# Another order of query tiles in a causal first pass, and weights before rows in the late expert slots of a decoder kernel

## The chip, the cores and the metric

The kernel runs on one core of a Trainium2 chip. A core has five engines with instruction streams of their own: TensorE (PE, matrix products; its weight loads are listed as PEld), VectorE (DVE), ScalarE (ACT), GpSimd (POOL) and SyncE (SP), which mostly issues DMA transfers. The streams are tied together by semaphores. The metric is the device time of one execution in microseconds, the median over runs.

## The reference, cut to what matters

Two decoder layers over `x` of shape 4 x 512 x 256, in float32. Layer 0: an attention over landmarks, an attention block, a quantised linear map. Layer 1: a hyperbolic attention, two further attentions with their own feed-forward nets, and a mixture of experts. Two pieces are touched by the change. The first is the causal half of layer 0's attention block (16 heads, queries and keys of 16 numbers, padded to 32 in the kernel):

```python
att = jnp.einsum('bhqd,bhkd->bhqk', q, k) * scale
causal = jnp.tril(jnp.ones((T, T), bool))
att = jnp.where(causal[None, None], att, -jnp.inf)
y = jnp.einsum('bhqk,bhkd->bhqd', jax.nn.softmax(att, axis=-1), v)
```

The second is the mixture of experts, in which each of 2048 tokens has its two best of eight experts:

```python
for e in range(NUM_EXPERTS):
    h = jax.nn.gelu(x @ W1[e] + b1[e])
    y = h @ W2[e] + b2[e]
    output = output + y * combine_w[..., e:e + 1]
```

## The kernel before, in words

**Attention as a stream of steps.** `Stream` (its `run`) works through *units*: one batch, one group of four heads, one kind. A unit has two passes. The first pass (`d_tile`) takes a tile of 128 queries against the keys (L386) and lets VectorE reduce the row maxima (L394 for causal units, L398 for the others). The second pass (`a_tile`) computes the scores again with keys as rows, the maxima already subtracted (L421), exponentiates them on ScalarE (L422) into `pt`, and a step later `outputs` multiplies them by the values (L517). One step of the stream holds one first-pass tile of one unit, one second-pass tile of an earlier unit, and the output products of the step before, in two halves. In a half, two heads of the first pass and two of the second are written out alternately; each head occupies 32 rows of TensorE, so the four stand in different row groups. The scores lie in a ring of seven PSUM banks.

In a causal unit the work narrows. Query tile `qt` of the first pass is `(qt + 1) * 128` keys wide; key tile `i` of the second pass is `512 - 128 * i` queries wide, with `i` from 0 to 3. Each batch of layer 0 has four cross units (eight steps, all 512 wide) and then four causal units (four steps each). The cross units set the distance between the passes: the second pass of a causal unit runs ten steps after its first pass. So of a batch's 16 causal steps of a first pass, ten meet a second pass of a cross unit and six meet one of a causal unit. Between them lie small pieces of work (projections, transposes, layer norms), placed by a planner with costs and due times; it doesn't look at widths.

**Experts by slots.** Tokens are scattered into `rows`, sorted by expert, by GpSimd's indirect DMAs (L1653). The products then go over 39 *slots* of 128 rows with one expert each. Slots 0 to 15 (`NEARLY = 16`) can be fixed once three batches are known, the other 23 only at the end, from a second table `tab1`. A slot needs its weights (`fetch_w`, L1809: 2052 KB into a pool of four buffers) and its rows (`fetch_z`, L1803: 128 KB into a pool of 16). `turn` transposes the rows (L1820, copied by L1822), `hidden` computes half of the first product (L1831) with its GELU (L1833), `output` the second product (L1838), which VectorE copies into `ys` (L1840) and SP stores (L1841). Before each fetch SP reads the expert or the row number from the table into a register.

`begin` asks for weights and rows of slots 0 to 2 and for rows of slots 3 to 15. Then `round` lays, for slot `s`: `fetch(s + 3)`, `hidden(s + 1)` twice, `turn(s + 2)`, `output(s)`. Rounds 0 to 12 are laid by `begin`, rounds 13 to 38 by `rest`, a second chain. The first piece of `rest`, `fetch(16)`, has no cost for the planner and is laid as soon as the second chain exists, in the middle of round 5. All these transfers are issued by SP, in program order on one queue; an instruction on SP that waits holds up those behind it. Order on TensorE is program order as well.

Of the kernel before, what the change touches and what calls it, by code (L numbers as in the profile page):

```python
# [23 lines left out]
NT = T // P  # L24
# [5 lines left out]
NEARLY = 16  # L30
VW = 16 * 17 + 15
NSLOT = 2 * B * T // P + E - 1
# [5 lines left out]
def decoder_kernel(ctx: ExitStack, tc: tile.TileContext, a: dict, out: bass.AP):  # L38
# [3 lines left out]
    def ts(i, n=P):  # L42
        return slice(i * n, (i + 1) * n)
# [34 lines left out]
    def ring():  # L78
        return banks["s"].tile([P, 512], F32, name="ps_s", tag="s")
# [227 lines left out]
    class Stream:  # L307
# [69 lines left out]

        def d_tile(self, u, i, j):
            if u.mode == "causal":
                qt, hf = NT - 1 - i, 0  # L380
                n = (qt + 1) * P
            else:
                qt, hf, n = i // u.halves, i % u.halves, 512
            r = ts(j, 32)
            ps = ring()
            PE.matmul(ps[:, 0:n], u.qT[r, ts(qt)], u.kT[r, hf * 512 : hf * 512 + n], start=True, stop=True)  # L386
            m = u.mx[:, qt, j, hf : hf + 1]
            if u.norm:

                V.tensor_reduce(m, ps[:, 0:n], AX.X, ALU.max, negate=True)  # L390
                self.open.append((ps[:, 0:n], m, u.sm[:, qt, j, hf : hf + 1]))
            elif u.mode == "causal":
                junk = self.one.tile([P, T], F32, name="junk", tag="junk")
                V.tensor_tensor_reduce(  # L394
                    junk[:, 0:n], ps[:, 0:n], self.dmask[:, T - n : T], 1.0, NEG, ALU.add, ALU.max, m
                )
            else:
                V.tensor_reduce(m, ps[:, 0:n], AX.X, ALU.max)  # L398
# [611 lines left out]
    def l1_attn(wo, spk, qk_d, v_d, left, done):  # L1010
        with ExitStack() as st:
# [173 lines left out]
            with tc.manual_schedule():  # L1185
                fetch(0, 0)
                n = len(units)
                prev_o = None
                for i in range(-1, n + 2):
                    u = units[i] if 0 <= i < n else None  # L1190
                    p = units[i - 1] if 0 <= i - 1 < n else None
                    nx = units[i + 1] if 0 <= i + 1 < n else None
                    if nx and nx.qts[0] == 2 and i >= 0:
                        k = 2 * nx.b + nx.hh + 1
                        if k < 2 * B:
                            fetch(k // 2, k % 2)
                    if p:
                        squares(p)
                    if u:
                        roots(u)  # L1200
                        pump()
                    if nx:
                        scores(nx)
                    if prev_o:
                        finish(*prev_o)
                        prev_o = None
                    if p:
                        prev_o = (p, outputs(p))
                    if u:
                        logs(u)  # L1210
# [474 lines left out]
    class Slots:  # L1685
# [123 lines left out]
            nc.sync.dma_start(u.w, a["we"][bass.ds(ex, 1)].rearrange("o p n -> p (o n)"))  # L1809

        def fetch(self, s):
            u = self.us[s]
            if s >= NEARLY:
                self.fetch_z(u)
            self.fetch_w(u)

        def turn(self, u):
            ps = ring()
# [203 lines left out]
```

## Time and profile before

| What | us |
|---|---|
| Median of 3 runs (lowest, highest) | 3512.26 (3512.18, 3515.68) |
| The profiled execution's own time | 3505.88 |
| Its span | 3504.0 |
| PE busy (share of the span) | 3055.5 (87%) |
| DVE busy | 2107.0 (60%) |
| ACT busy | 1901.9 (54%) |
| POOL busy | 781.5 (22%) |
| Causal first passes on VectorE (L394), first to last | 326.1 to 1081.4 |
| First fetch of an expert slot | 3093.3 |
| First and last product of the slots (L1831, L1838) | 3103.8, 3455 |

Times in the profile are microseconds from the start of the span. A row of the time line has start and length, the engine, the line of the kernel, the operation, what it writes and reads, and in brackets how long the engine had been idle and whose work ended that. Rows of PE are single hardware passes; a float32 product is two of them, so 32 passes of L1831 are the 16 products of both halves of `hidden`. SPq is SP's own queue: its rows are the issue of a transfer, and the landing is told apart. "PEclk" is the share of full clock that TensorE was granted.

### The profile page before, as it was taken

What the parts mean: (1) busy time and instruction counts of PE and PEld (TensorE: products, weight loads), DVE (VectorE), ACT (ScalarE), POOL (GpSimd) and SP (SyncE); (2) the same over time, 40 slices, a digit from 0 to 9 for tenths busy, and PEclk for the clock granted to TensorE, in tenths of its full rate; (3) what the DMA queues carried; (4) which work ended last, traced back from release to release, by engine and by line L of the source; (5) the groups of instructions that cost most, each with busy time, mean ns of one, the idle gap of its engine ahead of it and who ended that gap; (6) DMA issues with size and microseconds to landing.
All of it is one profiled execution on the core that took longest, in us unless ns stands there. A gap on an engine that the chain in (4) does not pass through costs nothing.

```text
span 3504.0 us, 50650 instructions
## 1 busy us (share of the span) xinstructions
PE 3055.5 (87%) x19095; PEld 1489.4 (43%) x19095; DVE 2107.0 (60%) x5076; ACT 1901.9 (54%) x3845; POOL 781.5 (22%) x667
## 2 busy tenths in 40 slices
PE   6689999999998576677899999999998998987994
PEld 3433333333333344344434444433333333457894
DVE  4576676776765677876776565655646656532112
ACT  2235555454553865879587667465663655532231
POOL 1010112122022745677222121100102001011003
PEclk9789999999999567777899999999998999999997
DMA  8100000010001100110000000000000000045895
GB/s 281 59 24 7 1 7 3 6 31 4 11 19 41 56 1 32 54 69 7 25 1 1 1 19 1 7 13 19 13 1 13 7 1 19 1 164 208 290 328 168
DMA packets 81397, 176.08 MB, mean 50 GB/s; under 512 B 6264, under 2 KB 63744, under 8 KB 76032
## 3 DMA queue, kind: packets, MB, share of 16 engines
q1 hardware_dynamic: 76016, 161.16, 13.1%
q0 software_dynamic: 3072, 8.39, 0.8%
q8 instruction: 150, 2.46, 0.3%
q10 hardware_dynamic: 2064, 3.29, 0.3%
q14 instruction: 95, 0.78, 0.1%
HBM read 127.48 MB, written 45.34 MB: 49 GB/s over the span
## 4 chain that ended last, share of the span: by engine, by line
PE 66%; DVE 13%; ACT 7%; issue 7%; DMA 5%; POOL 2%; SPq 0%; ACTq 0%; DVEq 0%; POOLq 0%
PE ps_s L386 16%; PE ps_g L517 7%; PE ps_s L421 5%; PE ps_s L661 3%; PE ps_s L1831 3%; PE ps_s L1838 3%; PE ps_s L1410 3%; PE ps_s L1356 3%; PE ps_s L1426 3%; PE ps_s L414 2%; PE ps_s L1145 2%; PE ps_g L524 2%; DMA rows<-ln_z,idx 1%; PE ps_s L1367 1%; DMA we<-in_we 1%
## 5 line engine op out<-in xcount | busy, mean ns | idle before, releaser
L422 ACT ACTIVATE pt<-ps_s 128x512 f32<-128x512 f32 (+2 forms) x1536 | 791.0, 569 | 749.0 <-PE ps_s L421 647.8
L386 PE MATMUL ps_s<-kT,qT 32*128 32x512 f32 (+3 forms) x3072 | 921.9, 623 | 45.6 <-ACT pt L422 28.0
L398 DVE TENSOR_REDUCE mx<-ps_s 128x1 f32<-128x512 f32 x768 | 489.3, 683 | 222.0 <-PE ps_s L386 124.8
L386 PEld LDWEIGHTS ps_s<-kT,qT 32*128 32x128 f32 x3072 | 310.9, 186 | 338.5 <-issue 96.4
L390 DVE TENSOR_REDUCE mx<-ps_s 128x1 f32<-128x512 f32 x512 | 328.3, 684 | 194.1 <-PE ps_s L386 190.9
L421 PE MATMUL ps_s<-qa,kT 32*128 32x512 f32 (+3 forms) x1536 | 436.0, 590 | 4.9 <-ACT pt L422 3.1
L421 PE MATMUL ps_s<-qT,kT 32*128 32x512 f32 x1536 | 417.6, 636 | 0.0
L402 ACT ACTIVATE ps_s<-ps_s,mx 128x512 f32<-128x512 f32 x512 | 340.9, 670 | 32.8 <-DVE mx L390 32.3
L1833 ACT ACTIVATE hid<-ps_s,we 128x128 f32<-128x128 f32 x312 | 88.9, 368 | 221.4 <-PE ps_s L1831 144.5
L1105 POOL TENSOR_TENSOR s<-s,mh 128x1280 f32<-128x1280 f32 x64 | 187.1, 2948 | 76.9 <-ACT mh L1104 57.1
L394 DVE CUSTOM_DVE_ANT_0 junk<-ps_s,dmask 128x512 f32<-128x512 f32 (+3 forms) x256 | 125.2, 489 | 95.8 <-PE ps_s L386 52.9
L1831 PE MATMUL ps_s<-zsT,we 128*128 128x128 f32 x1248 | 148.8, 278 | 22.7 <-DMA we<-in_we 20.6
L1088 PE MATMUL ps_s<-qk 32*128 32x256 f32 (+3 forms) x512 | 105.3, 628 | 65.6 <-DVE mh L1093 55.3
L421 PEld LDWEIGHTS ps_s<-qa,kT 32*128 32x128 f32 x1536 | 143.8, 185 | 42.7 <-DVE mx L398 24.0
L414 PE MATMUL ps_s<-qm,all 3*128 3x512 bf16 x768 | 156.6, 387 | 5.8 <-ACT ps_s L402 3.1
L164 POOL TENSOR_TENSOR ln_r<-ln_ve,mhalf 128x4 f32<-128x4 f32 x40 | 40.8, 1020 | 538.4 <-DVE ln_ve L159 476.0
L1831 PEld LDWEIGHTS ps_s<-zsT,we 128*128 128x128 f32 x1248 | 146.5, 194 | 28.0 <-issue 19.2
L1120 POOL TENSOR_TENSOR s<-s 128x1280 f32<-128x1280 f32 x64 | 147.6, 2337 | 12.3 <-ACT s L1116 12.3
L1147 DVE COPY pt<-ps_s 128x512 f32<-128x512 f32 x160 | 108.3, 687 | 58.7 <-PE ps_s L1145 58.7
L1145 PE MATMUL ps_s<-ident,s 128*128 128x128 f32 x640 | 127.7, 336 | 16.6 <-ACT s L1139 15.3
L1838 PE MATMUL ps_s<-we,hid 128*128 128x256 f32 x624 | 141.0, 379 | 0.0
L1093 DVE TENSOR_SCALAR_CACHE_REDUCE mh<-ps_s 128x512 f32<-128x512 f32 (+3 forms) x256 | 108.5, 486 | 53.1 <-PE ps_s L1092 28.8
(439 smaller groups left out, 5117.5 us busy)
## 6 DMA issues: line engine op xcount, KB each, us to landing
we<-in_we SPq DMA_DIRECT2D x39, 2052.0 KB, 8.8
rows<-zero SPq DMA_DIRECT2D x8, 2048.0 KB, 16.8
qk_d<-qkT SPq DMA_DIRECT2D x32, 256.0 KB, 2.7
qk<-qk_d SPq DMA_DIRECT2D x8, 1024.0 KB, 6.5
zs<-rows SPq DMA_DIRECT2D x39, 128.0 KB, 3.6
outs<-ys SPq DMA_DIRECT2D x39, 128.0 KB, 4.2
li<-in_a_li SPq DMA_DIRECT2D x4, 1024.0 KB, 8.7
v_d<-vp SPq DMA_DIRECT2D x16, 143.5 KB, 1.8
```

The source lines that it names most:

```text
L386: PE.matmul(ps[:, 0:n], u.qT[r, ts(qt)], u.kT[r, hf * 512 : hf * 512 + n], start=True, stop=True)
L390: V.tensor_reduce(m, ps[:, 0:n], AX.X, ALU.max, negate=True)
L398: V.tensor_reduce(m, ps[:, 0:n], AX.X, ALU.max)
L402: S.activation(ps, ps, AF.Exp, bias=m, accum_out=sm)
L414: PE.matmul(ps, self.ones[r, :], u.qm[r, :], start=True, stop=False)
L421: PE.matmul(ps[:, c0:], u.kT[r, ts(kt)], (u.qa if u.first_row else u.qT)[r, c0:], start=u.first_row, stop=True)
L422: S.activation(u.pt[:, j, c0:], ps[:, c0:], AF.Exp, scale=u.scale)
L517: PE.matmul(o[r, c0:], u.v(kt, j), pt[:, j, c0:], start=first, stop=last)
L1105: G.tensor_add(s, s, m)
L1145: PE.transpose(ps[:, ts(j)], u.s[h // 2][:, h % 2, c0 : c0 + P], ident)
L1831: PE.matmul(ps[:, ts(f)], u.w[:, k : k + P], u.zT[:, c, :], start=c == 0, stop=c == 1)
L1838: PE.matmul(ps[:, 0:C], u.h[:, f, :], u.w[:, 2048 + f * C : 2048 + f * C + C], start=f == 0, stop=f == 7)
```

## The change

In a causal unit, the first pass takes query tiles in the order 1, 0, 3, 2 instead of 3, 2, 1, 0, so its widths are 256, 128, 512, 384 instead of 512, 384, 256, 128. Ten steps later the second pass of that unit has 512, 384, 256, 128; in the steps where two causal units meet, both passes are now equally wide.

In the experts' stage, `fetch(s)` asks for the weights of slot `s` first. Then, for late slots only, it asks for the rows of slot `s - 1`; the call for the last slot asks for the rows of slots 37 and 38. The first call for a late slot, `fetch(16)`, asks for no rows at all: rows 16 come with weights 17.

```diff
         def d_tile(self, u, i, j):
             if u.mode == "causal":
-                qt, hf = NT - 1 - i, 0
+
+                qt, hf = (1 - i) % NT, 0
                 n = (qt + 1) * P
...
         def fetch(self, s):
-            u = self.us[s]
-            if s >= NEARLY:
+
+            self.fetch_w(self.us[s])
+            for u in self.us[max(s - 1, NEARLY) : s + (s == NSLOT - 1)]:
                 self.fetch_z(u)
-            self.fetch_w(u)
```

## The prediction

> **What bounds the kernel now.** I read the page first (busy tenths by slice), then the time line and the landings of the expert stage (3101 to 3457 us), then SP's waits, then the time line of the causal steps. TensorE is busy in nine tenths of most slices, and the DMA row rises only at the end:
>
> ```profile
> PE   6689999999998576677899999999998998987994
> DMA  8100000010001100110000000000000000045895
> ```
>
> In the rounds that handle late slots (16 to 38) nothing but TensorE sets the pace. Stretch of 160 us, columns: length, busy time of PE, PEld, DVE, ACT, POOL, granted clock, DMA share, GB/s:
>
> ```profile
> 3277.20:3437.30 160.10, 159.71 (x1100) 150.31 (x1101) 24.04 (x74) 50.21 (x176) 0.00 (x0) 1.00 0.89 320
> ```
>
> PE is busy 159.71 of 160.10 us: 22 rounds of 7.28 us. One of them on the time line:
>
> ```profile
> 3343.14 3.73 PE L1831 MATMUL ps_s<-zsT,we 128*128 128x128 f32 x32
> 3343.34 0.42 DVE L1840 COPY ys<-ps_s 128x256 f32<-128x256 f32 x1 [3.03 <-PE ps_s L1838]
> 3343.80 0.33 SPq L1841 DMA_DIRECT2D outs<-ys  x1
> 3344.91 0.34 SPq L1803 DMA_DIRECT2D zs<-rows  x1
> 3346.09 0.34 SPq L1809 DMA_DIRECT2D we<-in_we  x1
> 3346.71 0.38 PE L1820 MATMUL ps_s<-ident,zs 128*128 128x128 f32 x2
> 3346.93 3.62 PE L1838 MATMUL ps_s<-we,hid 128*128 128x256 f32 x16
> ```
>
> Call this round s. TensorE runs hidden(s+1), the row transposes turn(s+2), output(s). SP, once ys of slot s-1 is copied (3343.76), stores it, then asks for rows s+3 (1.15 us after the copy) and weights s+3 (2.33 us after). Rows s+3 are wanted a whole round later, so today their landing is hidden.
>
> **The change, part 1: late fetches.** The four compute engines execute the same instructions in the same order; SP issues as many, reordered. Round s now asks for weights s+3 first and then for rows **s+2**, which turn(s+2) wants in the same round. How long does a row transfer take behind a weight transfer? The first slots show it, from the views of the two tiles (weights issued at 3096.9, rows at 3098.0):
>
> ```profile
> L1809 SPq DMA_DIRECT2D we<-in_we x1: 338/338/338, 3096.9 to 3096.9; - x1
> DMA to landing us min/median/max: 12.7/12.7/12.7
> L1803 SPq DMA_DIRECT2D zs<-rows x1: 338/338/338, 3098.0 to 3098.0; - x1
> DMA to landing us min/median/max: 11.8/11.8/11.8
> ```
>
> Weights land at 3109.6, rows at 3109.8. The next rows, issued 1.1 us behind the next weights, land 0.4 us after them (3115.2 against 3114.8), and stores issued 0.4 us behind weights land 0.3 to 0.4 us after them (3245.4 against 3245.0). So 128 KB behind 2 MB land about 0.35 us after it; with nothing in front they take 1.9 to 2.1 us. Weights into an empty queue land after 7.7 to 9.5 us, mean 8.54.
>
> A rule of the Trainium skill speaks against me: "DMA: Bandwidth & Descriptors", section on queues, rings and completion order, says that completion on one issuing engine's queue isn't first in, first out. By it the rows could land after their own 2.0 us: copy 0, rows issued 2.33, landed 4.3, wake-up 0.1, then turn to end of copy 4.29: a round of 8.7 us, 22 x (8.7 - 7.3) = +31 us. By the rows above it is: weights issued 1.15, landed 9.69, rows 10.04, wake-up 0.1, plus 4.29 (turn start to end of the ys copy: 3353.96 to 3358.25 for the next slot) = 14.43 us a round, 22 x (14.43 - 7.31) = +157 us. I take the rows: this case has the very pair of transfers in the very order. Queued behind the waiting turn(s+2) is output(s); behind that the ys copy, its store, and on SP the next weights, which is why the wait isn't made up later. 7.31 is my count of the same 22 rounds in the trace (ends of copies 3277.0 to 3437.95).
>
> Which rounds: rows 16 are asked for with weights 17 in round 14, rows 37 with weights 38 in round 35: **22 stalled turns**; rows 38 follow at once.
>
> **The clock.** Each round leaves TensorE idle from the end of hidden(s+1) (3.0 us after the copy) to 10.1: 7.1 us. What such a gap does:
>
> ```profile
> 3212.00:3217.00 5.00, 0.00 (x0) 0.00 (x0) 0.42 (x1) 0.00 (x0) 0.00 (x0) 1.00 0.77 249
> 3217.20:3226.90 9.70, 0.01 (x1) 0.04 (x1) 0.00 (x0) 0.00 (x0) 0.00 (x0) 0.50 0.95 384
> 3226.90:3230.70 3.80, 3.80 (x18) 3.80 (x19) 0.00 (x0) 0.00 (x0) 0.00 (x0) 0.50 0.97 416
> ```
>
> The granted clock falls to 0.50 some 5 us into the gap and stays there 3.8 us after work resumes; the 32 hidden matmuls then took 5.67 us where 3.73 is usual. The ten gaps of over 4.3 us from 1987 us on all end in half clock, which lasts 3.2 to 9.0 us after resumption, mean 5.1. The rule in "TensorE: Matmul & The Clock Gate" (Part 1) counts a warm-up of about 3.4 us: 1.7 us lost per round, 22 x 1.7 = +37. By the rows' mean it is 2.5 us, +56. I take the rows, and round to the grid they show: switches lie 3.41 us or multiples of it apart, and half clock lasts one filled interval after the next switch point. As half of that is added to the round, the phase settles where a round is a whole number of intervals: five, 17.07 us (14.43 + 2.64; the rows' ends are 1.6 and 4.5, but for nine of the ten gaps 3.3). Late rounds: **22 x (17.07 - 7.31) = +215 us.**
>
> **What part 1 takes away.** Slot 16's fetch is laid early, in round 5, and today its rows wait for the last scatter of tokens, with everything on SP behind them:
>
> ```profile
> SPq L1803 <- DMA rows<-ln_z,idx: 19.6, 1, 19.6
> ```
>
> ```profile
> 3226.89 5.67 PE L1831 MATMUL ps_s<-zsT,we 128*128 128x128 f32 x32 [14.90 <-DMA we<-in_we]
> ```
>
> Behind them stood weights 16, the stores of ys 5 to 7 and weights 9 to 11; TensorE ran out of weights (14.90). Now only weights 16 stand there; they need output(5) (done 3195.4). Weights 9 go as soon as output(6) ends, 3204.75, land 3213.3, and hidden(9) starts at 3213.4, not 3226.9, without the half clock. What is late next: weights 16 hold one of four buffers, so slots 9 to 15 still cycle through three, each asked for at the end of an output and needed 7.44 us later against 8.54 to land. Stepping through gives hidden(15) at 3261.4 instead of 3277.2: **-15.8 us** (bounds -17 and -13, by weights landing in 8.3 or 9.0).
>
> **The change, part 2: causal order.** First-pass widths go from 512, 384, 256, 128 to 256, 128, 512, 384. The second pass lags ten steps, so only 6 steps of each batch pair two causal passes; elsewhere the partner is 512 wide. Row groups run side by side, so half a step costs the wider of its two:
>
> ```profile
> 380.34 0.69 PE L386 MATMUL ps_s<-kT,qT 32*128 32x512 f32 x1
> 380.34 0.48 PE L421 MATMUL ps_s<-qa,kT 32*128 32x256 f32 x1
> 381.40 0.85 PE L517 MATMUL ps_g<-pt,vs 128*32 128x384 f32 x8
> 384.70 0.58 PE L386 MATMUL ps_s<-kT,qT 32*128 32x384 f32 x1
> ```
>
> The half with 512 and 256 lasts 1.06 us (380.34 to 381.40), one with 384 and 128 lasts 0.85. Output blocks of 512, 384, 256 and 128 columns take 1.07, 0.85, 0.64 and 0.43 us: 0.21 per 128 columns. Paired 256 with 256 and 128 with 128, two steps of a batch lose 0.42 in each of two halves: 1.7 us, four batches 6.8. PE is busy 69.0 of 69.0 us there, so it counts. VectorE keeps up barely: 4 x 0.84 us in a 512 step, 0.71, 0.57, 0.44 in the others; the wide step now falls where PE has little else to do (3.2 us). I take **-4.5 us**, bounds -7 (no new wait) and +2 (0.4 us more waiting in the widest step of each of 16 units).
>
> **Sum.** -15.8 - 4.5 + 215 = +194.7 us. The profiled execution took 3505.88 us (span 3504.0, 1.9 around it), so 3700.6; the runs' median is 6.4 above it: **3707 us**.
>
> **Rivals.** (a) No clock loss, if the gate bridges 7 us: +157 - 20.3, **3649**; against it stands every gap over 4.3 us after 1987. (b) Rows pass the weights: +31 - 20.3, **3523**; against it stand the landings. (c) The other side: rows not only pass but land before TensorE has finished hidden(s+1), and the two gains remain: 3512.3 - 20.3 = **3492**. It decides at a loss of 20.3 / 22 = 0.92 us a round, that is at rows landing 1.6 us after issue; the shortest of the trace is 1.92. (d) Worse: weights landing in 9.5 us, or half clock for 2 us longer a round: rounds of 18 to 19 us, 22 x (10.7 to 11.7) - 20.3: **3727 to 3750**.
>
> **How the numbers follow.** Queue order with half clock 0.78, its own range 3683 to 3728; (a) 0.07; (b) 0.05; (c) 0.02; (d) 0.08. The range goes down to (a) and ends between the likeliest case and the bulk of (d): 3645 to 3732. Faster by over 0.2% (7 us, about what a measurement of this kernel can tell) has only (c): 0.02; within it, between (b) and (c): 0.02; slower 0.96.
>
> **What would show it.** Right: rows landing within 0.5 us of weights; turn waiting about 7 us on the rows' transfer in 22 rounds; rounds near 17 us, clock about 0.8 in that stretch; no 19.6 us wait before weights 16; PE halves of 0.64 and 0.43 in two causal steps per batch. Wrong: rows landing 2 to 3 us after issue, rounds of 14.4 us at full clock, or SP issuing weights ahead of ys.

## The result, and the profile after

The changed kernel takes **3694.15 us** (median of 6 runs, 3691.97 to 3702.73), the kernel before 3513.51 us (6 runs, 3511.41 to 3516.5): a ratio of 1.0516, interval 1.0503 to 1.053. The forecast was 3707 us, its range 3645 to 3732.

The page of the changed kernel, busy tenths in 40 slices and the granted clock:

```profile
PE   6699999999996676778999999999989898966553
PEclk9799999999996677778999999999999999987776
DMA  7200000000002001200000000000000004553343
```

The clock's row of the kernel before:

```profile
PEclk9789999999999567777899999999998999999997
```

The large differences lie in the last five slices (a slice is a fortieth of the span, 92 us here and 88 before, so the others shift a little). There TensorE, at 8, 7, 9, 9, 4 tenths before, falls to 6, 6, 5, 5, 3; the clock, at 9 before the last slice, falls to 8, 7, 7, 7, 6; and DMA, at 4, 5, 8, 9, 5 before, to 5, 3, 3, 4, 3. Nothing replaces TensorE as the bound: every engine waits. (Line numbers of the changed kernel are one higher than before from L386 on: turn L1821, hidden L1832, output L1839, copy of `ys` L1841, rows L1804, weights L1810.)

The same 22 rounds as in the prediction, from the copy of slot 13 to that of slot 35; columns: length, busy time of PE, PEld, DVE, ACT, POOL, granted clock, DMA share, GB/s:

```profile
3262.10:3626.40 364.30, 216.09 (x1102) 189.47 (x1101) 24.64 (x75) 50.37 (x176) 0.00 (x0) 0.75 0.40 144
```

PE executes the same matmuls (1102 here, 1100 before) in 364.30 us instead of 160.10. It is busy for 216.09 of them, against 159.71: the 56.4 us on top are the same products at half clock. The other 148.2 us are one and the same wait, once in each of the 22 rounds, as the group of the turn shows (busy time and mean ns, then idle time before and its releaser):

```profile
L1821 PE MATMUL ps_s<-ident,zs 128*128 128x128 f32 x78 | 21.1, 364 | 148.2 <-DMA zs<-rows 148.2
```

One round on the time line, the columns as before:

```profile
3376.71 3.73 PE L1832 MATMUL ps_s<-zsT,we 128*128 128x128 f32 x32
3376.91 0.42 DVE L1841 COPY ys<-ps_s 128x256 f32<-128x256 f32 x1 [5.41 <-PE ps_s L1839]
3377.36 0.33 SPq L1842 DMA_DIRECT2D outs<-ys  x1
3378.55 0.34 SPq L1810 DMA_DIRECT2D we<-in_we  x1
3379.66 0.34 SPq L1804 DMA_DIRECT2D zs<-rows  x1
3386.72 0.66 PE L1821 MATMUL ps_s<-ident,zs 128*128 128x128 f32 x2 [6.28 <-DMA zs<-rows]
3387.18 6.40 PE L1839 MATMUL ps_s<-we,hid 128*128 128x256 f32 x16
...
3393.61 0.42 DVE L1841 COPY ys<-ps_s 128x256 f32<-128x256 f32 x1 [5.77 <-PE ps_s L1839]
```

Copy ends at 3377.33, weights are asked for 1.2 us later, rows 2.3 us later; hidden is through at 3380.44, the turn starts at 3386.72, and the output products take 6.40 us where they took 3.62. The next copy ends at 3394.03: a round of 16.7 us, 7.2 before.

How long the two transfers take, from the views of the two tiles in these rounds; first the weights, then the rows:

```profile
L1810 SPq DMA_DIRECT2D we<-in_we x22: 337/338/348, 3263.3 to 3610.6; - x22
...
DMA to landing us min/median/max: 7.6/8.2/10.0
```

```profile
L1804 SPq DMA_DIRECT2D zs<-rows x23: 337/338/412, 3264.4 to 3612.8; - x23
...
DMA to landing us min/median/max: 6.8/7.3/8.0
```

Rows are issued 1.1 us behind the weights and take 0.9 us less: they land right behind them. In the 16 rounds of which the trace has both landings, rows land 0.29 to 0.35 us after the weights. By the ends of the copies, 22 rounds take 364.35 us (16.56 each) where they took 160.94 (7.32).

SP's waits between 3180 and 3262 us, while the slots 4 to 13 run (total, times, longest), which before held the 19.6 us on the scatter of tokens:

```profile
SPq L1810 <- PE ps_s L1839: 51.3, 8, 8.0
SPq L1842 <- DVE more L1698: 6.0, 1, 6.0
```

The wait on the scatter is gone; the longest of 8 us is at L1810, for a free weight buffer. The group of hidden between 3195 and 3262 us, first of the kernel before, then of the changed one:

```profile
L1831 PE MATMUL ps_s<-zsT,we 128*128 128x128 f32 x199 | 25.6, 290 | 17.7 <-DMA we<-in_we 17.7
```

```profile
L1832 PE MATMUL ps_s<-zsT,we 128*128 128x128 f32 x261 | 31.1, 277 | 6.0 <-DMA we<-in_we 6.0
```

TensorE waits 6.0 us for weights there instead of 17.7, and completes 261 single passes instead of 199.

Causal steps of the first batch, TensorE alone, in the changed kernel:

```profile
378.96 0.48 PE L387 MATMUL ps_s<-kT,qT 32*128 32x256 f32 x1
378.97 0.48 PE L422 MATMUL ps_s<-qa,kT 32*128 32x256 f32 x1
...
379.61 0.85 PE L518 MATMUL ps_g<-pt,vs 128*32 128x384 f32 x8
...
382.48 0.37 PE L387 MATMUL ps_s<-kT,qT 32*128 32x128 f32 x1
382.49 0.37 PE L422 MATMUL ps_s<-qa,kT 32*128 32x128 f32 x1
...
382.92 0.64 PE L518 MATMUL ps_g<-pt,vs 128*32 128x256 f32 x8
```

256 now meets 256 and 128 meets 128: the halves last 0.65 us (378.96 to 379.61) and 0.44 us (382.48 to 382.92), as the prediction had them (0.64, 0.43).

The spans of the two profiled executions, split where the prediction split them:

| Stretch | before | after | difference | forecast |
|---|---|---|---|---|
| start to hidden of slot 8 | 3204.58 | 3203.48 | -1.1 | -4.5 |
| hidden of slot 8 to hidden of slot 15 | 72.63 | 57.98 | -14.65 | -15.8 |
| hidden of slot 15 to the end | 226.79 | 431.04 | +204.25 | +215 |
| span | 3504.0 | 3692.5 | +188.5 | +194.7 |

Of the 204.25, 203.4 lie in the 22 rounds.

### The profile page after: what moved, and what is told of

It is laid out like the page before. It is cut to its first block, busy times and chain, and to the rows that moved or that the text cites. A ratio compares the mean times of both kernels' runs of the same rounds, so it can differ in the third digit from the quotient of the medians.

```text
span 3692.5 us, 50646 instructions
## 1 busy us (share of the span) xinstructions
PE 3111.2 (84%) x19095; PEld 1528.4 (41%) x19095; DVE 2110.1 (57%) x5076; ACT 1903.0 (52%) x3845; POOL 781.6 (21%) x667
## 4 chain that ended last, share of the span: by engine, by line
PE 63%; DVE 13%; DMA 8%; issue 7%; ACT 6%; POOL 2%; SPq 1%; ACTq 0%; DVEq 0%; POOLq 0%
PE ps_s L387 15%; PE ps_g L518 7%; PE ps_s L1839 5%; DMA zs<-rows 4%; PE ps_s L422 4%; PE ps_s L662 3%; PE ps_s L1411 3%; PE ps_s L1357 3%; PE ps_s L1427 3%; PE ps_s L415 2%; PE ps_s L1146 2%; PE ps_g L525 1%; PE ps_s L1368 1%; PE ps_s L1398 1%; PE ps_s L1832 1%
## 5 line engine op out<-in xcount | busy, mean ns | idle before, releaser
L391 DVE TENSOR_REDUCE mx<-ps_s 128x1 f32<-128x512 f32 x512 | 328.4, 684 | 194.7 <-PE ps_s L387 191.2
L1839 PE MATMUL ps_s<-we,hid 128*128 128x256 f32 x624 | 189.0, 471 | 0.0
L395 DVE CUSTOM_DVE_ANT_0 junk<-ps_s,dmask 128x256 f32<-128x256 f32 (+3 forms) x256 | 125.4, 490 | 93.8 <-PE ps_s L422 42.1
L1823 DVE COPY zsT<-ps_s 128x256 f32<-128x256 f32 x39 | 16.5, 422 | 271.7 <-PE ps_s L1821 271.7
L1839 PEld LDWEIGHTS ps_s<-we,hid 128*128 128x128 f32 x624 | 152.0, 250 | 28.2
L1832 PE MATMUL ps_s<-zsT,we 128*128 128x128 f32 x1248 | 148.5, 278 | 9.9 <-DMA we<-in_we 8.2
L1832 PEld LDWEIGHTS ps_s<-zsT,we 128*128 128x128 f32 x1248 | 146.3, 194 | 14.8 <-issue 8.8
L1821 PE MATMUL ps_s<-ident,zs 128*128 128x128 f32 x78 | 21.1, 364 | 148.2 <-DMA zs<-rows 148.2
```

The lines of the kernel that those rows point to most:

```text
L1832: PE.matmul(ps[:, ts(f)], u.w[:, k : k + P], u.zT[:, c, :], start=c == 0, stop=c == 1)
L1839: PE.matmul(ps[:, 0:C], u.h[:, f, :], u.w[:, 2048 + f * C : 2048 + f * C + C], start=f == 0, stop=f == 7)
```

## Experiments

The theory on record: rows queue directly behind 2 MB of weights that were asked for just before them, and a turn in the same round wants them. Its rivals: the wait is caused by one of the two edits inside `fetch` alone (order or delay); the clock makes most of the loss; the causal order takes part in it. Comparisons of the first four share 37 runs of the kernel before (median 3511.03), the last four share 11 (3512.86).

### The two parts apart

Causal order alone:

```diff
-                qt, hf = NT - 1 - i, 0
+                qt, hf = (1 - i) % NT, 0
```

> Only the causal order is changed. My theory (half a step costs the wider of its two row-group pairs): 1.2 to 1.7 us less in each of four batches, 4.7 us in all as the stream of steps showed it in the changed kernel, so 3509 us against 3513.5; at 1090 us from the start some 5 us ahead. Rival: the clock's switching grid gives it back later and the total is within 2 us of before. Second rival: VectorE's wider reductions where PE has little else cost as much as the pairing saves, and the stream itself shows under 2 us.

Measured: 3506.16 us (17 runs), ratio 0.9985 (0.9976 to 0.9994), or -4.9 us. The fetch edit alone, with the old causal order:

```diff
         def fetch(self, s):
-            u = self.us[s]
-            if s >= NEARLY:
+            self.fetch_w(self.us[s])
+            for u in self.us[max(s - 1, NEARLY) : s + (s == NSLOT - 1)]:
                 self.fetch_z(u)
-            self.fetch_w(u)
```

> Only the late fetches are changed. My theory: the two parts add up, so this costs all that the change cost and the causal gain besides: 22 rounds of 16.5 us (+203), 14.9 us less before them, 3513.5 + 188 = 3702 us. Rival: the parts interact (the causal order shifts the clock's phase for all that follows), and this is over 10 us from it.

Measured: 3699.85 us, ratio 1.0538 (1.0522 to 1.0554), or +188.8 us; 22 rounds of 16.47 us, the turns wait 145.5 us. The parts add up within the intervals: 188.8 - 4.9 = 183.9, the whole change is +180.6, and each of the three has an interval of 3 to 6 us to either side. The loss belongs to the fetch edit.

### Order or delay

The fetch edit does two things: weights go in front of rows, and rows are asked for a round later. Order without delay:

```diff
         def fetch(self, s):
             u = self.us[s]
+            self.fetch_w(u)
             if s >= NEARLY:
                 self.fetch_z(u)
-            self.fetch_w(u)
```

> Weights ahead of rows, but rows of the same slot (not one slot later): order changed, delay not. My theory: rows land 0.35 us behind weights, yet are wanted a round later, so no turn waits; rows 16 still hold SP up for the scatter, so that wait stays: 3513 us, within 4 us of before. Rival (a row transfer behind weights costs a stall by itself): 22 stalls of some 7 us, 3670 us or more.

Delay without order:

```diff
         def fetch(self, s):
-            u = self.us[s]
-            if s >= NEARLY:
+            for u in self.us[max(s - 1, NEARLY) : s + (s == NSLOT - 1)]:
                 self.fetch_z(u)
-            self.fetch_w(u)
+            self.fetch_w(self.us[s])
```

> Rows one slot later, but ahead of the weights: delay changed, order not. My theory: rows are issued 1.15 us after the ys copy and land 2.0 us later, 0.2 to 0.4 us after PE is through with the hidden products, so rounds of 7.6 us: 22 x 0.35 = +8; rows 16 no longer hold up SP, -14.9: 3506 us. Rival (the missing round of lead alone makes the stall): rounds over 12 us, 3620 us or more.

Measured: order alone 3513.95 us, ratio 1.001 (1.0001 to 1.0019); delay alone 3513.66 us, ratio 1.001 (1.0001 to 1.002). Each by itself costs some 3 us, both together 188.8. It is the pair that makes the wait: rows in the same round **and** behind the weights.

Delay alone came out 8 us above the 3506 us expected. It does gain the time of slots 8 to 13 (50.43 us between the copies of slots 7 and 13, 64.56 before), but its 22 rounds take 8.13 us each instead of the 7.6 expected, which gives 18 us back:

```profile
3262.91:3441.74 178.83, 164.17 (x1106) 151.46 (x1107) 24.55 (x75) 50.23 (x176) 0.00 (x0) 1.00 0.81 288
```

That stretch of "delay alone" (columns as above) has the full clock and 164.17 us of work in 178.83. The idle time is the turn's wait on its rows, at most 1.54 us each. The expectation took rows with nothing in front as landing 2 us after their issue. But the weights of the **previous** round are still in front of them. That can be read in the kernel before, whose rows are issued ahead of their own weights; here one transfer of weights and the rows issued after it:

```profile
L1809 SPq DMA_DIRECT2D we<-in_we x1: 338/338/338, 3324.7 to 3324.7; - x1
DMA to landing us min/median/max: 8.4/8.4/8.4
```

```profile
L1803 SPq DMA_DIRECT2D zs<-rows x1: 338/338/338, 3330.4 to 3330.4; - x1
DMA to landing us min/median/max: 3.3/3.3/3.3
```

Weights land at 3333.1, rows at 3333.7. In 14 of the 17 late rounds of that trace which have both landings, rows land 0.63 to 0.89 us after the weights of the round before; in the other three 1.1 to 2.1 us after. The trace of delay alone has no landing of a late transfer, but 21 of its turns wait for their rows; they start 9.7 us (mean) after the weights of the previous round were issued, against 8.8 + 0.65 + 0.1 = 9.55 by the kernel before. So rows wait for the weights in front whatever the round, and one sum covers all cases: from a copy on, weights issued, 8.8 us until they land (mean of the same rounds before), rows, 0.1 us of wake-up, 4.32 us from turn to the next copy, and this must fit into the number of rounds between asking and wanting. Delay alone: 2.33 + 8.8 + 0.65 + 0.1 + 4.32 = 16.2 us for two rounds, 8.1 each (measured 8.13). Order alone: 1.2 + 8.8 + 0.33 + 0.1 + 4.32 = 14.75 us for two rounds, 7.4 each, just above the 7.25 that TensorE needs (measured 7.52, waits of the turn of 0.2 to 1.0 us in six rounds). Both: 14.75 us for **one** round.

### The share of the clock

To keep the clock up, 13 products that nobody reads are put in front of each stalled turn; `fetch` and the causal order are those of the changed kernel:

```diff
         def turn(self, u):
+            if NEARLY <= u.s < NSLOT - 1:
+                ps = ring()
+                for k in range(13):
+                    PE.matmul(ps[:, 0:C], ident, x[:, 0, :], start=True, stop=True)
             ps = ring()
```

> The changed kernel with 13 products of no use ahead of each stalled turn (slots 16 to 37), about 5.9 us of TensorE in a gap of 6.1 to 7.3 us; the result is not touched. My theory: the clock stays full, the output's products run at full speed and a round is 1.15 + 8.1 + 0.33 + 0.1 + 4.29 = 14.0 us: 22 x (16.56 - 14.0) = 56 us less than the changed kernel, 3638 us. Rival: the clock is no part of the price (weights' landing alone sets the round): rounds stay at 16.5 us, 3694 us, or grow by what the added products delay.

Measured: 3660.05 us, ratio 1.0416 (1.04 to 1.0431), 22 us above the expectation. The 22 rounds (line numbers here: filling L1821, turn L1824, output L1842; weights L1809):

```profile
3262.63:3593.93 331.30, 294.38 (x1678) 261.68 (x1679) 24.67 (x75) 50.23 (x176) 0.00 (x0) 0.98 0.45 158
```

```profile
3372.81 5.78 PE L1821 MATMUL ps_s<-x,ident 128*128 128x256 f32 x26
3379.68 0.41 PE L1824 MATMUL ps_s<-ident,zs 128*128 128x128 f32 x2 [1.09 <-DMA zs<-rows]
3379.93 3.62 PE L1842 MATMUL ps_s<-we,hid 128*128 128x256 f32 x16
```

The clock is at 0.98, output is back at 3.62 us, and yet a round takes 15.06 us. Each round split at the start of its turn says why (means of 22 rounds):

| | copy to turn | turn to next copy | round |
|---|---|---|---|
| before | 3.01 | 4.31 | 7.32 |
| after | 9.85 | 6.72 | 16.56 |
| after, filled | 10.43 | 4.63 | 15.06 |

Filling takes 2.09 us from the second part, which leaves 0.3 us of the clock's loss. But it adds 0.58 us to the first: the turn still starts on the landing of the rows (the 1.09 us of wait in the row above), and the weights in front of them are slower:

```profile
DMA to landing us min/median/max: 8.1/8.7/9.8
```

The median is 8.7 us against 8.2 in the changed kernel; the means are 8.77 and 8.22. In the kernel before, where TensorE is busy too, it is 8.78. So the clock's share of the loss is 6.72 - 4.31 = 2.4 us a round, 53 us in all, of some 203; the rest is the wait itself.

### The bytes in front

If rows wait for what is in front, fewer bytes in front shorten the wait. Weights in two transfers, rows between them; else the changed kernel:

```diff
-            nc.sync.dma_start(u.w, a["we"][bass.ds(ex, 1)].rearrange("o p n -> p (o n)"))
+            src = a["we"][bass.ds(ex, 1)].rearrange("o p n -> p (o n)")
+            nc.sync.dma_start(u.w[:, 0:2048], src[:, 0:2048])
+            for v in between:
+                self.fetch_z(v)
+            nc.sync.dma_start(u.w[:, 2048:WROW], src[:, 2048:WROW])
```

> The changed kernel with each weight transfer cut in two, and the rows between the halves. My theory (rows land 0.35 us behind what stands before them in the queue): 1 MB in front lands after 5.3 us instead of 8.1, rows 6.8 us after the ys copy, turn to copy 4.29: 11.2 us a round at full clock, 12 to 13.5 with part of the output at half clock: 22 x 3 to 4.5 less, 3595 to 3630 us. Rival (rows take 7 us for another reason, such as reading rows from memory in that stage): rounds stay at 16 us or more, 3690 us.

Measured: 3614.76 us, ratio 1.0284 (1.0268 to 1.03), rounds of 13.42 us. The three transfers and the turn of one round (halves L1810 and L1813, rows L1803, turn L1822):

```profile
3356.41 0.34 SPq L1810 DMA_DIRECT2D we<-in_we  x1
3357.53 0.34 SPq L1803 DMA_DIRECT2D zs<-rows  x1
3358.06 0.33 SPq L1813 DMA_DIRECT2D we<-in_we  x1
3362.00 0.66 PE L1822 MATMUL ps_s<-ident,zs 128*128 128x128 f32 x2 [3.70 <-DMA zs<-rows]
```

The first half lands 5.0 us after its issue (3361.4), the rows 0.47 us later (3361.87), the turn follows at once. From copy to turn it is 7.16 us in the mean instead of 9.85: half the bytes, 2.7 us less. It is what stands in front that counts, not all that is under way: the second half of the weights was issued right behind the rows, and in the 12 landings that the trace has, rows land 0.3 to 1.1 us after the first half. Whether rows on the queue of another engine would wait as well was not tried. Gaps of 3.6 to 5.5 us still trip the clock, in 20 of 22 rounds (6.25 us from turn to copy). An effect that was not forecast: slots 8 to 13 now come at TensorE's own pace, 43.97 us between the copies of slots 7 and 13. The products of hidden read only the first half of the weights, and there it lands 5.9 to 7.6 us after its issue, the second half after 7.8 to 9.5.

### What was good in the change

Two kernels keep the causal order and the old `fetch`, and take only what part 1 took away. In the first, rows 16 are asked for behind weights 15, so the early call for slot 16 asks for weights alone:

```diff
             u = self.us[s]
-            if s >= NEARLY:
+            if s > NEARLY:
                 self.fetch_z(u)
             self.fetch_w(u)
+            if s == NEARLY - 1:
+                self.fetch_z(self.us[NEARLY])
```

> The causal order, and of the late fetches only this: rows 16 are asked for behind weights 15 instead of with weights 16, all others as before the change. My theory: SP no longer stands still for the scatter in front of weights 9 to 11 (-14 to -15 us), no turn waits, causal -4.7: 3494 us. Rival: the wait for the scatter is hidden anyway or comes back as slower weights in slots 9 to 15: over 3505 us.

In the second, all of slot 16's fetch moves to its own place behind round 12:

```diff
-            return head + self.round(0, NEARLY - 3)
+            return head + self.round(0, NEARLY - 3) + [(0.0, lambda: self.fetch(NEARLY))]
...
-            work = self.round(NEARLY - 3, NSLOT)
-            work.insert(12, (0.5, self.places))
+            work = self.round(NEARLY - 3, NSLOT)[1:]
+            work.insert(11, (0.5, self.places))
```

> The causal order, and the whole fetch of slot 16 moved from round 5, where the planner laid it, to its own place behind round 12, rows ahead of weights as before. My theory: SP doesn't wait for the scatter, and four weight buffers instead of three serve slots 9 to 15, so these take 7.25 us each instead of 10.8 (64.6 us from copy 7 to copy 13 become 43.5): -21, causal -4.7: 3488 us. Rival: the fourth buffer gives nothing, since weights are then limited by the transfers: 3494 us as with rows 16 alone.

Measured: 3494.33 us, ratio 0.9947 (0.9933 to 0.996), and **3485.96 us**, ratio 0.9918 (0.9903 to 0.9933), the fastest of these kernels. The end of the early slots (copies of slots 5 to 13) and then the 22 rounds of the second one:

```profile
3195.00:3257.10 62.10, 62.10 (x421) 57.84 (x420) 8.60 (x19) 18.31 (x64) 5.75 (x6) 1.00 0.82 291
3257.10:3417.14 160.04, 159.66 (x1102) 150.22 (x1102) 24.48 (x75) 50.39 (x176) 0.00 (x0) 1.00 0.90 325
```

TensorE is busy in 62.10 of 62.10 us. From copy 7 to copy 13 it takes 64.56 us before, 51.23 with rows 16 moved, 43.47 with all of slot 16 moved: weights 16, fetched early, hold one of four buffers, and that costs 7.8 us more, which the changed kernel pays too. SP's waits in front of a weight transfer (L1809) between 3180 and 3262 us, first with rows 16 moved, where they end with the products of output (there L1840) that free a weight buffer, then with all of slot 16 moved, where hardly any is left:

```profile
SPq L1809 <- PE ps_s L1840: 54.1, 8, 9.4
```

```profile
SPq L1809 <- PE ps_s L1831: 0.9, 5, 0.2
```

Faster transfers are not the reason: of the weights issued in these slots, the first kernel's land after 8.5 to 9.5 us (five recorded), the second's after 7.8 to 10.5 (seven), four of them after more than 10. The late rounds keep 7.34 and 7.27 us.

## Why the prediction was right

**Queue order: right, every round.** The prediction took a pair of landings of the first slots for the rule. It set aside what the Trainium skill says ("DMA: Bandwidth & Descriptors", section on queues, rings and completion order): that completion on one issuing engine's queue is not first in, first out. In the changed kernel rows land 0.29 to 0.35 us after the weights, forecast 0.35; 22 turns wait, forecast 22. Rival (b) would have had rounds of 8.7 us, rival (c) would have had no wait. What the page says of completion in general no run here contradicts; that the rows could land after 2.0 us of their own was the prediction's reading of it, and no late round of the changed kernel shows that.

**Size of the wait: 0.3 us too long.** Copy to turn was forecast as 1.15 + 8.54 + 0.35 + 0.1 = 10.14 us and is 9.85. The term is the landing of the weights, 8.2 us instead of 8.54: the 8.54 came from rounds with a busy TensorE, and the filled kernel brings the slower landing back. 22 x 0.29 = 6 us.

**Clock: right in kind, 0.2 us too much.** Forecast 4.29 + 2.64 = 6.93 us from turn to copy, measured 6.72. The step that failed is that "the phase settles where a round is a whole number of intervals: five": rounds of 17.04 to 17.14 us occur (seven of 22), but others take 14.99 to 16.99, one 17.47. The clock in the round shown above, from the end of hidden on (columns as above):

```profile
3380.50:3382.60 2.10, 0.00 (x0) 0.00 (x0) 0.00 (x0) 1.13 (x4) 0.00 (x0) 0.99 0.91 375
3382.60:3386.60 4.00, 0.00 (x0) 0.00 (x0) 0.00 (x0) 0.00 (x0) 0.00 (x0) 0.50 0.71 295
3386.80:3393.20 6.40, 6.40 (x18) 5.18 (x19) 0.42 (x1) 0.00 (x0) 0.00 (x0) 0.53 0.01 3
```

The clock falls 2.1 us into the gap, not 5 us as in the gap shown before, and stays down for 6.1 us after work resumes (3386.72 to 3392.8). The half clock lasts 6.83 or 10.24 us, two or three of the trace's intervals of 3.41 us, and where the gap falls on that grid decides. In 18 of the 22 rounds it ends as the forecast had it, one filled interval after the next switch point; in the other four it ends one interval sooner, 2.9 to 3.0 us after work resumes, and three of these are the rounds of 15.0 to 15.1 us. The mean loss of 2.4 us (53 us) lies at the 2.5 us (56) that the rows of before gave, above the 1.7 us (37) that the prediction had estimated from the warm-up in the Trainium skill's "TensorE: Matmul & The Clock Gate", Part 1.

**Taken away in slots 9 to 15: -14.65 for -15.8.** The wait on the scatter is gone, and hidden of slot 15 starts at 3261.46 us (forecast 3261.4); but slot 8 was by then 1.1 us ahead, so the stretch itself gained less. The term is again the landing of weights: three of those recorded took 9.4 to 10.0 us, not 8.54. "Rows 16 moved" alone confirms the cause: 13.6 us less than the causal order alone (-18.5 against -4.9).

**Causal order: right where it acts, not all kept in this execution.** From the first causal step's reduction on VectorE to the last one's, over all four batches, it is 755.06 us before and 750.36 after: 4.7 us gained, 4.5 forecast; and the causal order alone gives -4.9 us in the median. All ten traces agree: this stretch takes 755.05 to 755.09 us in the four with the old order and 750.13 to 750.42 in the six with the new one. (TensorE's 69.0 busy us of 69.0, from which the forecast took that the pairing counts in full, are the first batch's; in the last it is 70.9 of 74.) The forecast had nothing for what follows: from the last of these reductions to one and the same step of the second passes (at 1093 us before), the four take 11.7 us and the six 10.1, another 1.6 us gained. In the trace of before TensorE is at half clock there until 1083.8 us, for 2.7 us of it; whether that is all of it was not tried.

The changed kernel's execution was 8.1 us ahead at 1093 us (1.8 of them from before the first causal step), 5.2 at 2095 and 1.1 at slot 8. The 2.9 us lost up to 2095 are within what this stretch, in which no instruction differs, varies by itself: 998.6 to 1005.4 us in the four traces with the old order. 3.3 us went between 2095 and 2189 us, where no instruction differs either. There a gap of TensorE of the same length met another phase of the clock's grid. The 10 us after the gap, first before, then after:

```profile
2142.00:2152.00 10.00, 9.65 (x58) 6.44 (x57) 5.18 (x13) 6.35 (x18) 5.99 (x4) 1.00 0.00 1
```

```profile
2137.00:2147.00 10.00, 9.65 (x50) 6.15 (x49) 4.46 (x11) 5.30 (x15) 5.72 (x4) 0.84 0.00 1
```

Both have PE busy for 9.65 us, one at full clock with 58 passes, the other at 0.84 with 50. Half clock lasted 10.24 and a further 3.41 us instead of 6.83. The edit is not the cause: of the ten traces two take 94.04 us between these points (before, and delay alone), the other eight 97.33 to 97.36, and two of the eight, the fetch edit alone and order alone, have the old causal order.

**The sum.** Of the 13 us between 3707 and 3694, 6.2 come from these terms (+3.4 causal, +1.15 slots 9 to 15, -10.75 late rounds). The other 6.8 are the step from one execution to the median: before, the profiled execution lay 6.4 us under the median and the prediction carried that over; after, it lies 0.4 us above (3694.53).

## What to carry to other kernels

Count what stands in front of a small transfer on its queue, and how many rounds lie between asking and wanting: weights issued + their landing + rows + use must fit into that number of rounds, and the same swap costs some 3 us with two rounds and 189 us with one. A fetch that is asked for early holds a buffer early: moving slot 16's whole fetch to its turn was worth 22.0 us over the causal order alone, removing only its wait 13.6. Where a wait of several us recurs on TensorE, add the clock's share from gaps of the same trace (here 2.4 us per gap of 6.7), but don't expect the rounds to settle on the clock's grid.

## What the runs showed of the hardware

- Rows land behind the weights of the previous round as well, 0.63 to 0.89 us after them, even when asked for 5.7 to 7.0 us later and ahead of their own. In the kernel before this was there all along, hidden by a round of slack; a median landing of 3.6 us in the late rounds, where an empty queue gave 1.9 to 2.1, was the sign.
- The 2052 KB of weights land after 8.22 us in the mean while TensorE idles between asking and landing, and after 8.77 us when it is kept busy with products that need no transfer. The filled kernel shows the effect; its cause stays open.
- The phase of the clock's grid moves work that no edit touches: 3.3 us at one gap of the same length, two values over ten traces. One profiled execution can hide a gain of 5 us that 17 runs show: the profiled execution of the causal order alone has a span of 3507.0 us, 3 us longer than before, though its causal stretch is 4.7 us shorter. The stretch itself tells what the span does not.
